# Last graph layer on column tiles of 32, with the mixing stage between the groups

## The chip, the cores and the metric

The kernel runs on one core of one Trainium2 chip. The metric is the device time of one execution in microseconds (us). Before the change the median of three runs is 4722.29 us (4718.48 to 4723.53). The engines are named as the profile does: PE is the matmul engine and PEld its weight loads, DVE is VectorE, ACT is ScalarE, POOL is GpSimd, SP issues DMAs. "PEclk" is the share of full speed that was granted to PE.

## The reference

A network of four layers over 3125 nodes with 256 features each. Every layer adds a graph part and a mixing part to x, and then an expert part. The change is in the last layer's graph part, which runs together with that layer's mixing part:

```python
def _L3_gnn_ref(x, edge_index, W, att_src, att_dst):      # 4 heads of 64 columns
    xp = (x @ W).reshape(n, 4, 64)
    a_src = jnp.einsum('nhc,hc->nh', xp, att_src)
    a_dst = jnp.einsum('nhc,hc->nh', xp, att_dst)
    e = leaky_relu(a_src[src] + a_dst[dst], 0.2)
    e_exp = jnp.exp(e - segment_max(e, dst)[dst])
    alpha = e_exp / segment_sum(e_exp, dst)[dst]
    return relu(segment_sum(alpha[:, :, None] * xp[src], dst).reshape(n, 256))

def _L3_mix_ref(x, Wq, Wk, Wv, Wm, W1, W2, g1, b1, g2, b2):
    Q, K = elu(q) + 1, elu(k) + 1                         # 8 heads of 32
    msg = layernorm(linear_attention(Q, K, v) @ Wm, g1, b1)
    h = relu(concat([x, msg]) @ W1) @ W2
    return x + layernorm(h, g2, b2)

xn = layernorm(x)
x = x + _L3_gnn_ref(xn, edge_index, ...) + _L3_mix_ref(xn[None], ...)[0]
x = x + _L3_ffn_ref(layernorm(x), ...)                    # one of 8 experts per node
```

## The kernel before

The nodes are 25 blocks of 125 (P), and also seven pieces (PIECES): six of 500 nodes (PW) and one of 125. `self.x`, `self.xn` and `self.xt` hold x, the normalised x, and the latter with features on partitions, for the whole network.

The graph part is done densely. Earlier, the kernel has written to HBM, for every piece of target nodes, a bf16 matrix of how often each source node points to each target (`ctt_d`). With exponentials taken apart into a factor of the source and one of the target, the weight of a source block for a stretch of targets is one ACT instruction and one DVE instruction: `t` = Relu(rows x scale + bias) on line 1951, and `z` = (t + us) x count on line 1954. `rows` holds, for each head, the targets' factor, the same on all partitions; `us` holds three factors of each source.

`l3_gnn_mix` (line 1834) sets this up. It makes the 64 columns of each head for each source block (`xr`, with a 65th column of ones, so that a product also gives the sum of the weights), the attention terms `al`, the bias, and `us`. It then runs two generators side by side in `together` (line 1892): `l3_dense`, the graph part, and `l3_mix_by_pieces`, the mixing part. At each turn the generator that is less far along goes on, so the program text of the two is interleaved in small steps. A scheduler then orders each engine's instructions by priority and readiness, mainly in that order[...].

`l3_dense` (line 1902) goes over four groups of pieces: three of two pieces (1000 targets) and the last piece alone. For each group

- it makes `rows`: for each head and piece two matmuls of a broadcast column of `wx` with `xt` (line 1930), and an Exp from PSUM into `xn`'s space (line 1932);
- for two heads at a time (for the last piece all four) it goes over the 25 source blocks. It loads the block's counts (`cs`, three buffers, two DMAs on SP, lines 155 and 156), makes `t` (two buffers) and `z` (three buffers) for each head, and issues one product per head and piece on line 1957: stationary `xr` (125 x 65), moving `z` (125 x 500), summed up in one PSUM bank per head and piece, four banks in all;
- it copies the four banks to SBUF, transposes them block by block (line 1972), and `finish` divides by the sum and adds the Relu to x with five DVE instructions per block and pair of heads (lines 1912 to 1919).

[...]

`l3_mix_by_pieces` (line 1990) first does keys and values of the 25 blocks (`keys_values`, lines 1270 to 1300), and then for each piece: queries, attention (line 1318), its normalising on DVE (lines 1322 to 1325), a transpose (line 1337), the product with Wm (line 254), a layer norm (`norm_piece`), a transpose (line 2021), W1 (line 2030), W2, a second layer norm, and the sum into x. Each piece needs several passes from PE to DVE or ACT and back.

When both parts of a piece are done, `arrive` starts its routing (`follow` in `l3_ffn`, line 2185): norm, transposes, gate products, softmax, slots, and a scattered write to HBM. The experts read this back after the last piece.

Of the kernel before, what the change touches and what calls it, by code (L numbers as in the profile page):

```python
# [12 lines left out]
F32 = mybir.dt.float32  # L13
# [4 lines left out]
AF = mybir.ActivationFunctionType  # L18
OP = mybir.AluOpType
# [4 lines left out]
N = 3125  # L24
D = 256
P = 125
NB = 25
HB = D // 128
# [9 lines left out]
PW = 500  # L38
# [67 lines left out]
PIECES = [(i, min(PW, N - i)) for i in range(0, N, PW)]  # L106


class Net:
# [1724 lines left out]
    def l3_gnn_mix(self, before, arrivals):  # L1834
# [5 lines left out]
        nc, a = self.nc, self.a  # L1840
        with ExitStack() as s:
            ms = s.enter_context(self.pool("m3_sb"))
            with self.pool("m3_w") as sb:
                w = self.load_w(sb, "L3_gnn_W")
                wx = self.attn_cols(sb, w, "wx", ["L3_gnn_att_src", "L3_gnn_att_dst"], ms)
            mix = self.l3_mix_by_pieces(ms, None)
# [4 lines left out]
            sb = s.enter_context(self.pool("g3_sb"))  # L1851
            wk = s.enter_context(self.pool("g3_wk", 2))
            pa = s.enter_context(self.pool("g3_ps", 1, space=PSUM))
            xr = sb.tile([P, NB, 4, 65], F32, name="xr")
            nc.gpsimd.memset(xr[:, :, :, 64:65], 1.0)
            al = sb.tile([P, NB, 8], F32, name="al")
            for b in range(NB):
                ps = self.bank()
                self.mm_tok(ps[:P, :264], self.xt, b, wx)
                nc.vector.tensor_copy(xr[:, b, :, :64], ps[:P, :D].rearrange("p (h d) -> p h d", h=4))  # L1860
                nc.scalar.copy(al[:, b, :], ps[:P, 256:264])
            m = sb.tile([P, 8], F32, name="m")
            nc.vector.tensor_reduce(m, al.rearrange("p b h -> p h b"), axis=AX.X, op=OP.max)
            ps = self.bank()
# [5 lines left out]
            ps = self.bank()  # L1870
# [4 lines left out]
            bias = sb.tile([P, 4], F32, name="bias3")  # L1875
# [5 lines left out]
            nc.vector.tensor_reduce(self.viol[:P, 6:7], over, axis=AX.X, op=OP.add)  # L1881
            nc.vector.tensor_tensor(bias, a8, bias, op=OP.min)

            us = sb.tile([P, 3, NB, 4], F32, name="us")
            nc.vector.tensor_sub(us[:, 2], al[:, :, :4], top[:, :, :4].to_broadcast([P, NB, 4]))
            nc.scalar.activation(us[:, 0], us[:, 2], AF.Exp)
            nc.scalar.activation(us[:, 1], us[:, 2], AF.Exp, scale=0.2)
            nc.vector.tensor_scalar(us[:, 2], us[:, 1], -1.0, None, op0=OP.mult)
            mix.send(mw)
            self.together([self.l3_dense(sb, wk, pa, wx, xr, us, bias), mix], (1.0, 1.15))  # L1890

    def together(self, parts, pace=(1.0, 1.0)):

# [5 lines left out]
            except StopIteration:  # L1899
                del at[p]  # L1900

    def l3_dense(self, sb, wk, pa, wx, xr, us, bias):

        nc = self.nc
        few = sb.tile([P, NB, 4], F32, name="few")
        free = self.xn.rearrange("p b d -> p (b d)")
        rows = free[:, :8 * PW].rearrange("p (h d) -> p h d", h=4)
        at = free[:65, 8 * PW:12 * PW].rearrange("p (h d) -> p h d", h=2)

        def finish(b, h0, nh, acc):  # L1910

            nc.vector.tensor_scalar(few[:, b, h0:h0 + nh], acc[:, :, 64], 1e-20, None, op0=OP.is_lt)
            rd = wk.tile([P, 4], F32, name="rd")
            nc.vector.tensor_scalar(rd[:, :nh], acc[:, :, 64], 1e-20, None, op0=OP.max)
            nc.vector.reciprocal(rd[:, :nh], rd[:, :nh])
            t = wk.tile([P, 4, 64], F32, name="tf")
            nc.vector.tensor_mul(t[:, :nh], acc[:, :, :64], rd[:, :nh, None].to_broadcast([P, nh, 64]))
            v = self.x[:, b, h0 * 64:(h0 + nh) * 64]
            nc.vector.scalar_tensor_tensor(v, t[:, :nh].rearrange("p h d -> p (h d)"), 0.0, v,
                                           op0=OP.max, op1=OP.add)  # L1920

        done, there = 0, []
        for p0 in range(0, len(PIECES), 2):
            pcs = PIECES[p0:p0 + 2]
            n = sum(w for _, w in pcs)
            for h in range(4):
                for k, (i, w) in enumerate(pcs):
                    ps = self.bank()
                    for c in range(HB):
                        nc.tensor.matmul(ps[:P, :w], wx[:, c, 260 + h:261 + h].to_broadcast([128, P]),  # L1930
                                         self.xt[:, c, i:i + w], start=(c == 0), stop=(c == HB - 1))
                    nc.scalar.activation(rows[:, h, k * PW:k * PW + w], ps[:P, :w], AF.Exp, bias=bias[:, h:h + 1],
                                         scale=0.8)
            hg = 4 if n < PW else 2
            for h0 in range(0, 4, hg):
                acc = {}
                for h in range(hg):
                    for k in range(len(pcs)):
                        acc[h, k] = pa.tile([65, 512], F32, name=f"acc{h * len(pcs) + k}")
                for b in range(NB):  # L1940
                    cs = wk.tile([P, 2, PW], BF, name="cs", bufs=3)
                    if len(pcs) == 2:
                        self.move(nc.sync, cs, self.ctt_d[p0:p0 + 2, :, b, :].rearrange("k p d -> p k d"))
                        c = cs.rearrange("p k d -> p (k d)")
                    else:
                        self.move(nc.sync, cs[:, 0, :n], self.ctt_d[p0, :, b, :n])
                        c = cs[:, 0, :n]
                    for h in range(hg):
                        k4 = h0 + h
                        t = wk.tile([P, 2 * PW], F32, name="t5")  # L1950
                        nc.scalar.activation(t[:, :n], rows[:, k4, :n], AF.Relu, bias=us[:, 2, b, k4:k4 + 1],  # L1951
                                             scale=us[:, 0, b, k4:k4 + 1])
                        z = wk.tile([P, 2 * PW], F32, name="z", bufs=3)
                        nc.vector.scalar_tensor_tensor(z[:, :n], t[:, :n], us[:, 1, b, k4:k4 + 1], c,  # L1954
                                                       op0=OP.add, op1=OP.mult)
                        for k, (i, w) in enumerate(pcs):
                            nc.tensor.matmul(acc[h, k][:, :w], xr[:, b, k4, :], z[:, k * PW:k * PW + w],  # L1957
                                             start=(b == 0), stop=(b == NB - 1))
                        done += n
# [5 lines left out]
                if hg == 2:  # L1965
                    for h in range(2):
                        for k, (i, w) in enumerate(pcs):
                            self.evac(at[:, h, k * PW:k * PW + w], acc[h, k][:, :w])
                    for j in range(n // P):
                        ps = self.bank()  # L1970
                        for h in range(2):
                            nc.tensor.transpose(ps[:P, h * 65:(h + 1) * 65], at[:, h, j * P:(j + 1) * P],
                                                self.ident[:65, :65])
                        finish(p0 * 4 + j, h0, 2, ps[:P, :130].rearrange("p (h c) -> p h c", h=2))
                        yield done / (NB * N * 4)
                else:
                    for h in range(4):
                        self.evac(at[:, h // 2, h % 2 * P:(h % 2 + 1) * P], acc[h, 0][:, :P])
                    ps = self.bank()
                    for h in range(4):  # L1980
                        nc.tensor.transpose(ps[:P, h * 65:(h + 1) * 65], at[:, h // 2, h % 2 * P:(h % 2 + 1) * P],
                                            self.ident[:65, :65])
                    finish(p0 * 4, 0, 4, ps[:P, :260].rearrange("p (h c) -> p h c", h=4))
# [426 lines left out]
```

## Time and profile before

| | |
|---|---|
| median of three runs | 4722.29 us |
| profiled execution | 4857.34 us, span 4855.5 us, mean PE clock 0.859 |
| PE busy in the span | 3791.1 us (78%) |
| DVE, ACT, POOL busy | 2518.8 (52%), 1321.2 (27%), 1016.0 us (21%) |
| product of the graph part, L1957 | first 3695.3, last 4586.5 us |
| t on ACT, L1951 | 400, median 1220 ns for 1000 columns |
| z on DVE, L1954 | 400, median 1258 ns for 1000 columns |
| cs loads | 150 of 218.8 KB and 150 of 25.4 KB for two pieces |

A time in a view is counted from the span's start. The page's groups give, for one line, engine and shape, the summed busy time, the mean duration of one, and the idle time before it with what ended it. Ends of matmuls are modelled and overlap the next one's start, so two neighbouring matmuls can have a mean duration that is longer than the distance between their starts. The stage of the change is the last fifth but one of the span; what follows it is the experts' stage.

### The profile page before, as it was taken

To read this page: it belongs to the slowest core of one execution; us is meant where nothing else is said; L and a number is where in the kernel's file an instruction comes from. 1 tells how busy PE (TensorE), PEld (TensorE's weight loads), DVE (VectorE), ACT (ScalarE), POOL (GpSimd) and SP (SyncE) were. 2 spreads that over 40 slices of the span, in tenths; PEclk is the share of its full clock that TensorE was granted. 3 is DMA by queue.
4 is the path that set the end of the run, shared out by engine and by line. 5 is a ranking of instruction groups with operands and counts; after the bars stand their busy time and mean duration, and the time that the engine had idled before them with its cause. 6 is when DMAs were issued, how large, how long until landed. Compare 5 with 4: busy or idle time off the path is not lost. (4 is left out here: it accounts for less than half of the span.)

```text
span 4855.5 us, 50596 instructions
## 1 busy us (share of the span) xinstructions
PE 3791.1 (78%) x16806; PEld 2521.4 (52%) x16806; DVE 2518.8 (52%) x8603; ACT 1321.2 (27%) x2364; POOL 1016.0 (21%) x1041
## 2 busy tenths in 40 slices
PE   1886895799657899997454556676599999999798
PEld 0675894566534565555343445455364444444465
DVE  5886335445576319954222222343355667667544
ACT  1466100111123232333000000000154655556511
POOL 1000002200243000002666666666000000000011
PEclk8786996799878799998676777787799999999799
DMA  6245511433230000002333333333301112111132
GB/s 181 59 119 145 137 33 40 127 119 118 82 80 19 24 14 7 14 7 65 90 94 92 93 92 92 86 93 92 111 7 31 51 44 59 42 49 52 50 128 68
DMA packets 253461, 352.56 MB, mean 73 GB/s; under 512 B 61645, under 2 KB 198276, under 8 KB 253191
## 3 DMA queue, kind: packets, MB, share of 16 engines
q1 hardware_dynamic: 133326, 169.77, 12.1%
q0 software_dynamic: 62832, 126.93, 9.9%
q10 hardware_dynamic: 57033, 52.54, 4.0%
q8 instruction: 137, 2.24, 0.2%
q14 instruction: 133, 1.09, 0.1%
HBM read 262.48 MB, written 94.92 MB: 74 GB/s over the span
## 5 line engine op out<-in xcount | busy, mean ns | idle before, releaser
L1598 POOL DMA_INDIRECT hg<-hx_d,idx x782 | 743.0, 950 | 418.8 <-issue 209.7
L1614 PE MATMUL acc<-hg,to 128*125 128x256 f32 x2042 | 590.7, 445 | 280.7 <-issue 157.7
L1614 PEld LDWEIGHTS acc<-hg,to 128*125 128x125 f32 x2042 | 439.3, 222 | 411.1 <-issue 192.7
L1957 PE MATMUL acc<-z,xr 125*65 125x500 f32 (+1 forms) x1400 | 573.7, 552 | 10.5 <-DVE z L1954 8.6
L1609 DVE TENSOR_SCALAR to<-iota_w,rel_b,kw 128x125 f32<-128x125 f32 (+1 forms) x782 | 252.7, 378 | 454.9 <-remote 263.6
L1954 DVE SCALAR_TENSOR_TENSOR z<-t,us,cs 125x1000 f32<-125x1000 f32 (+1 forms) x400 | 410.2, 1029 | 136.2 <-PE acc L1957 103.3
L1951 ACT ACTIVATE t<-xn,us 125x1000 f32<-125x1000 f32 (+1 forms) x400 | 409.4, 1037 | 236.9 <-DVE z L1954 231.3
L1957 PEld LDWEIGHTS acc<-z,xr 125*65 125x65 f32 x1400 | 187.8, 143 | 313.2 <-issue 271.3
L260 PE MATMUL ps<-xt,w 128*128 128x500 f32 (+1 forms) x672 | 268.8, 547 | 1.8 <-DMA w<-in_L_ffn_W_dram 1.8
L1533 DVE SCALAR_TENSOR_TENSOR junk<-iota_w,rel_b,lock 128x125 f32<-128x125 f32 (+1 forms) x782 | 248.0, 384 | 0.0
L796 ACT ACTIVATE k<-k 125x128 f32<-125x128 f32 x50 | 15.8, 317 | 775.1 <-DVE k L795 542.8
L2240 POOL DMA_INDIRECT bx_d<-row,slot x25 | 31.2, 1247 | 923.3 <-ACT t L1951 809.4
L588 PE MATMUL ps<-y,cb 125*125 125x256 bf16 x1875 | 215.2, 280 | 0.0
L588 PEld LDWEIGHTS <-cb 125*125 125x125 bf16 x1875 | 214.0, 141 | 0.1
L189 ACT ACTIVATE rstd_t<-rstd_t 125x4 f32<-125x4 f32 (+2 forms) x86 | 17.2, 203 | 678.6 <-DVE rstd_t L188 622.1
L254 PE MATMUL ps<-wo,h 128*125 128x256 f32 x800 | 187.7, 386 | 3.6 <-ACT h L1436 2.6
L1442 DVE SCALAR_TENSOR_TENSOR x<-ps,lg,x 125x256 f32<-125x256 f32 x200 | 92.7, 480 | 173.5 <-PE ps L254 173.5
L260 PEld LDWEIGHTS ps<-xt,w 128*128 128x128 f32 x672 | 122.7, 193 | 114.5 <-issue 102.2
L260 PE MATMUL ps<-h,w 128*128 128x500 f32 (+1 forms) x448 | 179.5, 541 | 2.3 <-ACT h L1431 1.6
L254 PEld LDWEIGHTS ps<-wo,h 128*125 128x125 f32 x800 | 142.7, 187 | 66.0 <-ACT h L1436 43.7
L260 PE MATMUL pl<-xbt,w 128*128 128x384 f32 x416 | 169.9, 557 | 8.2 <-DVE xbt L1152 5.8
L469 PE MATMUL t<-ky,lo 128*128 128x75 bf16 (+4 forms) x1251 | 138.5, 253 | 38.6 <-ACT ct L472 24.5
(566 smaller groups left out, 6225.3 us busy)
## 6 DMA issues: line engine op xcount, KB each, us to landing
cs<-ctt_d SPq DMA_DIRECT2D x150, 218.8 KB
w<-in_L_ffn_w_dram SPq DMA_DIRECT2D x52, 512.0 KB
cnt_d<-cd SPq DMA_DIRECT2D x25, 683.6 KB
cb<-cnt_d SPq DMA_DIRECT2D x25, 683.6 KB
ctt_d<-ct ACTq DMA_DIRECT2D x6, 2734.4 KB
hg<-hx_d,idx POOLq DMA_INDIRECT x782
b0x_d<-zero SPq DMA_DIRECT2D x1, 9984.0 KB
xb<-b0x_d SPq DMA_DIRECT2D x26, 384.0 KB
```

What stands on the lines that cost most here:

```text
L254: self.nc.tensor.matmul(ps, xt[:, h, b * P:(b + 1) * P], w[:, h, :], start=(h == 0), stop=(h == k - 1))
L260: self.nc.tensor.matmul(ps, w[:, h, :], xt[:, h, i:i + n], start=(h == 0), stop=(h == k - 1))
L469: nc.tensor.matmul(t[:, w * 25 * r:(w + 1) * 25 * r], lo[:, :, n % 4], ky[:, :25 * r, n % 4], start=(j == 0), stop=(j == ws[w0 + w][2] - 1))
L588: nc.tensor.matmul(ps[:P, :D], cf[k][:, h * P:(h + 1) * P], y3[:, b0 + k, j, :], start=(k == 0 and j == 0), stop=(k == m - 1 and j == 2))
L1442: nc.vector.scalar_tensor_tensor(self.x[:, b, :], ps[:P, :D], g[:, b, e:e + 1], self.x[:, b, :], op0=OP.mult, op1=OP.add)
L1533: nc.vector.scalar_tensor_tensor(junk[:, :m * P], self.iota_w[:, :m * P], rel[:, c:c + 1], lock[:, b:b + m].rearrange("p b n -> p (b n)"), ...
L1598: nc.gpsimd.indirect_dma_start(out=hg[:, j, :], out_offset=None, in_=hx, in_offset=bass.IndirectOffsetOnAxis(ap=idx[:, c0 + j:c0 + j + 1], ...
L1609: nc.vector.tensor_scalar(to, self.iota_w[:, :nb * P], rel[:, c:c + 1], kw[:, j:j + 1], op0=OP.is_equal, op1=OP.mult)
L1614: nc.tensor.matmul(acc[k], to[:, (k - b) * P:(k - b + 1) * P], hg[:, j, :D], start=(c == first[k]), stop=(c == last[k]))
L1951: nc.scalar.activation(t[:, :n], rows[:, k4, :n], AF.Relu, bias=us[:, 2, b, k4:k4 + 1], scale=us[:, 0, b, k4:k4 + 1])
L1954: nc.vector.scalar_tensor_tensor(z[:, :n], t[:, :n], us[:, 1, b, k4:k4 + 1], c, op0=OP.add, op1=OP.mult)
L1957: nc.tensor.matmul(acc[h, k][:, :w], xr[:, b, k4, :], z[:, k * PW:k * PW + w], start=(b == 0), stop=(b == NB - 1))
```

## The change

Seven things change, all in `l3_gnn_mix` and `l3_dense`.

1. `xr` has 64 columns; the column of ones goes. Each product is cut into tiles of 32 columns: for one source block, two heads and two pieces, eight products of 32 feature columns and four of 32 columns of ones (the sums). Each names its column tile with `tile_position=(0, q)`, q = 0, 32, 64, 96 in turn, and writes partitions q to q + 31 of a PSUM bank: one bank per piece (two heads of 64 columns), and one bank for the four sums.
2. These twelve products are chained with `add_manual_dep`, each after the one before it and the first after the block's `z`, and issued with `high_priority(5000)`. On PE the blocks of a group then follow one another; in the order of the changed kernel's instructions nearly all mixing and routing work stands between the groups.
3. A group takes three of four accumulator banks, turning on by three each time.
4. `rows` is no longer made on PE. Four Exp instructions on `al`, one transpose and one copy make the factors of all targets, which are written to HBM (`r_d`, 4 x 3125) and read back by broadcast, in `target_rows`: both head pairs ahead of the first group, and later each pair as soon as the group before has issued its last block.
5. `t` moves from its own two buffers to two stretches of `xn`'s space; `z` has four buffers in place of three; `at`, where results are copied, gets its own buffer.
6. The results are transposed as 128 x 125 tiles, four blocks to a bank, and `finish` works on four blocks at once.
7. The last piece, 125 targets wide, has all four heads in one group, also as twelve products of 32 columns per block.

```diff
-            xr = sb.tile([P, NB, 4, 65], F32, name="xr")
-            nc.gpsimd.memset(xr[:, :, :, 64:65], 1.0)
+            xr = sb.tile([P, NB, 4, 64], F32, name="xr")
...
+            r = sb.tile([P, 4, NB], F32, name="r3")
+            for h in range(4):
+                nc.scalar.activation(r[:, h], al[:, :, 4 + h], AF.Exp, bias=bias[:, h:h + 1], scale=0.8)
+            ps = self.bank()
+            nc.tensor.transpose(ps[:4 * NB, :P], r.rearrange("p h b -> p (h b)"), self.ident[:P, :P])
+            rt = sb.tile([4 * NB, P], F32, name="rt3")
+            nc.vector.tensor_copy(rt, ps[:4 * NB, :P])
+            r_d = self.dram.tile([4, N], F32, name="r3_d")
+            nc.sync.dma_start(r_d.rearrange("h (b p) -> (h b) p", p=P), rt)
...
+        spare = [free[:P, j * PW:(j + 2) * PW] for j in (8, 10)]
+        groups = [PIECES[p:p + 2] for p in range(0, len(PIECES), 2)]
+
+        def target_rows(g, h0):
+            if g < len(groups):
+                i, n = groups[g][0][0], sum(w for _, w in groups[g])
+                for h in (h0, h0 + 1):
+                    self.move(nc.sync, rows[:P, h, :n], r_d[h, i:i + n].partition_broadcast(P))
+
+        def finish(b, nb, h0, nh, acc):
+            w, nu = nb * P, len(acc) - 1
+            at = wk.tile([128, 3, PW], F32, name="at", bufs=1)
+            for k in range(nu + 1):
+                self.evac(at[:, k, :w], acc[k][:, :w])
...
+                for j in range(nb):
+                    nc.tensor.transpose(ps[:P, j * 128:(j + 1) * 128], at[:, k, j * P:(j + 1) * P], self.ident)
+                t = wk.tile([P, 4, 2, 64], F32, name="tf")
+                nc.vector.tensor_mul(t[:, :nb], ps[:P, :nb * 128].rearrange("p (j h d) -> p j h d", j=nb, d=64),
+                                     rd[:, :nb, 2 * k:2 * k + 2, None].to_broadcast([P, nb, 2, 64]))
...
-            for h in range(4):
-                for k, (i, w) in enumerate(pcs):
-                    ps = self.bank()
-                    for c in range(HB):
-                        nc.tensor.matmul(ps[:P, :w], wx[:, c, 260 + h:261 + h].to_broadcast([128, P]),
-                                         self.xt[:, c, i:i + w], start=(c == 0), stop=(c == HB - 1))
-                    nc.scalar.activation(rows[:, h, k * PW:k * PW + w], ps[:P, :w], AF.Exp, bias=bias[:, h:h + 1],
-                                         scale=0.8)
...
+            for hs in ((0, 2),) if len(pcs) == 1 else ((0,), (2,)):
+                units = [(h0, k, w) for h0 in hs for k, (_, w) in enumerate(pcs)]
+                acc = [pa.tile([128, 512], F32, name=f"acc{(turn + j) % 4}") for j in range(3)]
+                turn += 3
...
+                    zs, made = {}, made[-1:]
+                    for h in [h0 + j for h0 in hs for j in range(2)]:
+                        t = spare[h % 2]
+                        nc.scalar.activation(t[:, :n], rows[:P, h, :n], AF.Relu, bias=us[:, 2, b, h:h + 1],
+                                             scale=us[:, 0, b, h:h + 1])
+                        z = zs[h] = wk.tile([P, 2 * PW], F32, name="z", bufs=4)
+                        made.append(nc.vector.scalar_tensor_tensor(z[:, :n], t[:, :n], us[:, 1, b, h:h + 1], c,
+                                                                   op0=OP.add, op1=OP.mult))
-                        for k, (i, w) in enumerate(pcs):
-                            nc.tensor.matmul(acc[h, k][:, :w], xr[:, b, k4, :], z[:, k * PW:k * PW + w],
-                                             start=(b == 0), stop=(b == NB - 1))
+                    with self.tc.high_priority(5000):
+                        for out, left, h0, j, k, w, q in (
+                                [(acc[u], xr[:, b, h0 + j, f:f + 32], h0, j, k, w, 64 * j + f)
+                                 for u, (h0, k, w) in enumerate(units) for j in range(2) for f in (0, 32)]
+                                + [(acc[2], self.ones[:P, :32], h0, j, k, w, 64 * u + 32 * j)
+                                   for u, (h0, k, w) in enumerate(units) for j in range(2)]):
+                            mm = nc.tensor.matmul(out[q:q + 32, :w], left, zs[h0 + j][:, k * PW:k * PW + w],
+                                                  start=(b == 0), stop=(b == NB - 1), tile_position=(0, q))
+                            for i in made:
+                                self.tc.add_manual_dep(mm.ins, i.ins.name, row, reason="in one row")
+                            made = [mm]
...
+                for h0 in hs:
+                    target_rows(g + 1, h0)
+                finish(b0, pcs[0][1] // P, hs[0], 2 * len(hs), acc)
```

More of the change, by code (lines that the diff above doesn't have):

```diff
@@ L1859, in l3_gnn_mix @@
                 self.mm_tok(ps[:P, :264], self.xt, b, wx)
[L1860 removed]
+                nc.vector.tensor_copy(xr[:, b], ps[:P, :D].rearrange("p (h d) -> p h d", h=4))
                 nc.scalar.copy(al[:, b, :], ps[:P, 256:264])
@@ L1889, in l3_gnn_mix @@
             mix.send(mw)
-            self.together([self.l3_dense(sb, wk, pa, wx, xr, us, bias), mix], (1.0, 1.15))
+            self.together([self.l3_dense(sb, wk, pa, xr, us, r_d), mix], (1.0, 1.15))
     def together(self, parts, pace=(1.0, 1.0)):
@@ L1900, in together, with l3_dense @@
                 del at[p]
-    def l3_dense(self, sb, wk, pa, wx, xr, us, bias):
+    def l3_dense(self, sb, wk, pa, xr, us, r_d):
         nc = self.nc
@@ L1907, in l3_dense @@
         rows = free[:, :8 * PW].rearrange("p (h d) -> p h d", h=4)
[L1908 to L1920, printed above, removed]
@@ L1922, in l3_dense @@
-        done, there = 0, []
-        for p0 in range(0, len(PIECES), 2):
-            pcs = PIECES[p0:p0 + 2]
-            n = sum(w for _, w in pcs)
-            for h in range(4):
-                for k, (i, w) in enumerate(pcs):
-                    ps = self.bank()
-                    for c in range(HB):
-                        nc.tensor.matmul(ps[:P, :w], wx[:, c, 260 + h:261 + h].to_broadcast([128, P]),
-                                         self.xt[:, c, i:i + w], start=(c == 0), stop=(c == HB - 1))
-                    nc.scalar.activation(rows[:, h, k * PW:k * PW + w], ps[:P, :w], AF.Exp, bias=bias[:, h:h + 1],
-                                         scale=0.8)
[L1934 to L1939, printed above, removed]
+        spare = [free[:P, j * PW:(j + 2) * PW] for j in (8, 10)]
@@ new lines, in l3_dense @@
+        groups = [PIECES[p:p + 2] for p in range(0, len(PIECES), 2)]
[9 more added lines that the diff above has]
+                self.evac(at[:, k, :w], acc[k][:, :w])
+            ps = self.bank()
+            for j in range(nb):
+                nc.tensor.transpose(ps[:P, j * 128:(j + 1) * 128], at[:, nu, j * P:(j + 1) * P], self.ident)
+            sums = ps[:P, :nb * 128].rearrange("p (j q r) -> p j q r", j=nb, r=32)[:, :, :, 0]
+            rd = wk.tile([P, 4, 4], F32, name="rd")
+            f = wk.tile([P, 4, 4], F32, name="fw")
+            nc.vector.tensor_scalar(f[:, :nb], sums, 1e-20, None, op0=OP.is_lt)
+            nc.vector.tensor_scalar(rd[:, :nb], sums, 1e-20, None, op0=OP.max)
+            nc.vector.reciprocal(rd[:, :nb], rd[:, :nb])
+            for k in range(nu):
+                bk, hk = (b + 4 * k, h0) if nh == 2 else (b, 2 * k)
+                nc.vector.tensor_copy(few[:, bk:bk + nb, hk:hk + 2], f[:, :nb, 2 * k:2 * k + 2])
+                ps = self.bank()
+                for j in range(nb):
+                    nc.tensor.transpose(ps[:P, j * 128:(j + 1) * 128], at[:, k, j * P:(j + 1) * P], self.ident)
+                t = wk.tile([P, 4, 2, 64], F32, name="tf")
+                nc.vector.tensor_mul(t[:, :nb], ps[:P, :nb * 128].rearrange("p (j h d) -> p j h d", j=nb, d=64),
+                                     rd[:, :nb, 2 * k:2 * k + 2, None].to_broadcast([P, nb, 2, 64]))
+                v = self.x[:, bk:bk + nb, hk * 64:hk * 64 + 128]
+                nc.vector.scalar_tensor_tensor(v, t[:, :nb].rearrange("p j h d -> p j (h d)"), 0.0, v,
+                                               op0=OP.max, op1=OP.add)
@@ new lines, in l3_dense @@
+        done, there, turn, made = 0, [], 0, []
+        row = mybir.DependencyInfo(mybir.DependencyClass.NoSync, mybir.DependencyReason.DATA)
+        for h0 in (0, 2):
+            target_rows(0, h0)
+        for g, pcs in enumerate(groups):
+            b0 = pcs[0][0] // P
+            n = sum(w for _, w in pcs)
+            for hs in ((0, 2),) if len(pcs) == 1 else ((0,), (2,)):
+                units = [(h0, k, w) for h0 in hs for k, (_, w) in enumerate(pcs)]
+                acc = [pa.tile([128, 512], F32, name=f"acc{(turn + j) % 4}") for j in range(3)]
+                turn += 3
@@ L1942, in l3_dense @@
                     if len(pcs) == 2:
-                        self.move(nc.sync, cs, self.ctt_d[p0:p0 + 2, :, b, :].rearrange("k p d -> p k d"))
+                        self.move(nc.sync, cs, self.ctt_d[2 * g:2 * g + 2, :, b, :].rearrange("k p d -> p k d"))
                         c = cs.rearrange("p k d -> p (k d)")
                     else:
-                        self.move(nc.sync, cs[:, 0, :n], self.ctt_d[p0, :, b, :n])
+                        self.move(nc.sync, cs[:, 0, :n], self.ctt_d[2 * g, :, b, :n])
@@ L1947, in l3_dense @@
                         c = cs[:, 0, :n]
[L1948 to L1955, printed above, removed]
-                        for k, (i, w) in enumerate(pcs):
-                            nc.tensor.matmul(acc[h, k][:, :w], xr[:, b, k4, :], z[:, k * PW:k * PW + w],
-                                             start=(b == 0), stop=(b == NB - 1))
-                        done += n
+                    zs, made = {}, made[-1:]
@@ L1960, in l3_dense @@
+                    done += n * 2 * len(hs)
                     yield done / (NB * N * 4)
@@ L1964, in l3_dense @@
                         there = []
[L1965 to L1983, printed above, removed]
+                for h0 in hs:
+                    target_rows(g + 1, h0)
+                finish(b0, pcs[0][1] // P, hs[0], 2 * len(hs), acc)
+                yield done / (NB * N * 4)
             there = [i for i, w in pcs]
```

## The prediction

> **What bounds the kernel now.** The chain that ended last is no help here: it accounts for only some 7% of the span and breaks off inside the expert stage. So I read where TensorE (PE) is full (part 2 of the page), then the stage of the change by windows, then its groups with shapes kept apart, then single stretches of the timeline.
>
> ```profile
> PE   1886895799657899997454556676599999999798
> ...
> PEclk8786996799878799998676777787799999999799
> ```
>
> From slice 31 (3690 us) PE is full and its clock granted. The stage begins on PE at 3676.4, after L1871, and ends at 4610.2, at the first expert transpose. Columns below: stretch, its length, then busy us (instructions) of PE, PEld, DVE, ACT, POOL, PE clock, DMA share, GB/s.
>
> ```profile
> 3676.40:4610.20 933.80, 884.98 (x2771) 407.74 (x2771) 611.96 (x1335) 540.84 (x677) 31.18 (x25) 0.96 0.18 48
> 3690.00:4500.00 810.00, 796.71 (x2414) 353.41 (x2413) 543.29 (x1049) 471.94 (x536) 20.45 (x16) 1.00 0.19 50
> 4500.00:4610.20 110.20, 75.97 (x332) 48.93 (x331) 65.89 (x277) 63.21 (x131) 10.73 (x9) 0.70 0.16 42
> ```
>
> Up to 4500, PE idles 13 us in 810 at full clock, VectorE (DVE) is at 67%, ScalarE (ACT) at 58%: PE decides. After 4500 little dense work is left and 34 us are idle.
>
> ```profile
> L1957 PE MATMUL acc<-z,xr 125*65 125x500 f32 x1200 | 527.4, 583 | 2.8 <-DVE z L1954 2.8
> L1957 PE MATMUL acc<-z,xr 125*65 125x125 f32 x200 | 46.2, 367 | 7.7 <-DVE z L1954 5.8
> ...
> L1930 PE MATMUL ps<-xt,wx 128*125 128x500 f32 x78 | 36.3, 626 | 0.6 <-DVE rd L1914 0.6
> ...
> L1972 PE MATMUL ps<-ident,xn 65*125 65x65 f32 x96 | 15.1, 268 | 5.8 <-DVE few L1912 3.0 <-DVE rd L1914 1.3 <-DVE tf L1917 0.6
> ```
>
> The program has 700 products, the trace 1400 matmuls: each f32 product runs as two instructions, one behind the other. Their mean of 583 ns overlaps the next, so the price is the spacing:
>
> ```profile
> 4464.35 47.95 PE L1957 MATMUL acc<-z,xr 125*65 125x500 f32 x114
> ...
> 4470.77 2.64 DVE L1954 SCALAR_TENSOR_TENSOR z<-t,us,cs 125x1000 f32<-125x1000 f32 x2
> ```
>
> 47.95/114 = 0.42 us, so a product is 0.84 us and a block of two heads and two pieces (four products) 3.36 us. Where nothing holds DVE up, two z take 2.64 us: today they wait for PE.
>
> By spacing, the stage's 885 us of PE are: 150 full blocks x 3.36 = 504; 25 blocks of the last piece x 1.85 (46.2/25) = 46; rows of L1930, 96 x 0.42 + 16 x 0.21 = 44; 100 result transposes at 0.15 = 15; the remaining 276 are mixing and routing, which today fill gaps between dense products.
>
> **What the Trainium skill says.** "TensorE: Matmul & The Clock Gate", Part 3 (Measured speedup vs the span model): column tiles run side by side, three tiles with N=512 gave 2.38x, four row tiles 3.07x. The same part (What overlaps and what doesn't): matmuls start and end strictly in order. "TensorEngine Tiling (Array Packing)", Key Properties: a change of tiling mode drains TensorE. No run here shows tiles yet. The first page, HAM oscillation, lets PE's clock fall after pauses above about 3.4 us; the trace agrees: the first-layer mixing, which runs PE with pauses (14.27 us is the longest before L1337), had
>
> ```profile
> 1485.00:1540.00 55.00, 33.79 (x137) 22.42 (x137) 35.02 (x156) 15.93 (x28) 14.29 (x12) 0.84 0.08 17
> 1540.00:1600.00 60.00, 46.36 (x191) 33.25 (x190) 40.69 (x140) 15.46 (x27) 0.00 (x0) 0.72 0.00 1
> 1600.00:1670.00 70.00, 52.72 (x201) 37.25 (x200) 33.19 (x122) 18.58 (x33) 0.31 (x1) 0.67 0.14 42
> ```
>
> **The change part by part.**
>
> *Tiles.* A block becomes twelve products of 32 columns (eight of features, four of sums), issued to column tiles 0, 32, 64, 96 in turn: three rounds of four. If four run at once, a round costs one product: 3 x 0.84 = 2.51 us on PE. DVE then needs 2.64 for its two z, ACT 2 x 1.22 = 2.44, so DVE becomes the bound: 150 x 2.64 = 396, 108 less than 504. Bounds: 2.51 (PE alone) to 2.75 (t and z take turns on two buffers and their hand-over costs a little), that is -20 to +17 us. No row shows 24 weight loads of 32 columns in a block; the nearest spacing of load plus matmul is L469's 138.5 us/1251 = 0.11 us, so 24 x 0.11 = 2.66, no more than DVE. That tiles run at once is the assumption on which everything rests.
>
> *Last piece.* Its 25 blocks also become 24 short instructions: between 1.8 us (DVE's four z, 2 x 0.91 in the timeline near 4545) and 2.66. I take 2.3: 57 us against 46, +11.
>
> *Rows.* L1930's matmuls (44 us of PE), 28 Exp evictions and four table loads (5.1 us) on ACT go. In their place: four small Exp, one transpose, a copy, a 50 KB write and 16 broadcast reads (32 transfers, most rows 500 KB) through DRAM on SP's queue, read from r_d. At the 189 GB/s of 4600 to 4640 such a row takes 2.6 us. The first pair should be there at about 3690, while PE does six key-value blocks (2.25 us each, as in the first layer) that it had to do anyway: no loss. At later groups the reads wait for the last t of the group and stand ahead of the next cs loads on SP: 1.5 us of issue plus 1 MB, about 7 us, beside mixing work everywhere but between the first two groups. If mixing did not cover it: 5 x 7 = 35 us.
>
> *Results.* 100 transposes become 75 larger ones, 15 to 11 us; DVE's five small operations a block become few wide ones (some 20 us less, off the path). The fourth accumulator bank lets the next group start its first unit at once.
>
> *Order.* This is the cost. The instruction order of the changed kernel shows the 25 blocks of a group as one unbroken row on PE, and in the row DVE and ACT have almost only z and t. Mixing and routing stand between the groups: nothing after the first group but three key-value blocks, then thirteen, then whole pieces. There PE waits for each softmax, norm and copy, which before were hidden. What that costs is not in the trace; nearest is the first-layer mixing with routing, from 1506.0 to 1671.6: 166 us for work that at full-clock spacings (from the timeline, instructions x us) is about 97 (48 x 0.42 + 8 x 0.13, 100 x 0.222, 100 x 0.146, 100 x 0.13, 100 x 0.12, 25 x 0.15, 50 x 0.21), clock loss included: 11 us a piece of 500. The last layer's piece has two norms more. The first is on PE's path: statistics 0.6, two DVE steps, a table load 1.28, a root 0.2, four scalings of 0.54, about 4.6 us, and then a clock that may have fallen. I take 18 us a piece, 6.25 pieces: 113. Between 11 (70 us) and 25 (160 us). The start-up of t and z at six groups (6 x 2.5 us) about cancels with what still lies inside the rows of groups four, six and seven.
>
> *Sum.* PE 396 + 57 + 276 + 11 = 740; the 34 us of idle at the end stay; waits 113: 887 us against 934, -47 us. The profiled execution (4857.34 us: span 4855.5 and 1.84 around it) would become 4810. The median of the runs is 135 us lower; this stage was at full clock under the profiler, so I take the 47 off unscaled: **4675 us**. With its bounds (-43/+47 from the waits, -20/+17 from the block): 4615 to 4740.
>
> **The rivals.**
>
> *Pairs are not split (slower).* A product is two instructions on the same tile. If starts are strictly in order, the second waits for the first on its tile and holds back the next tile's; then only the tail of one product and the head of the next overlap, and each product costs 0.42. A block is 12 x 0.42 = 5.03 us: 150 x 2.39 = 358 more, 7 on the last piece: +318, 5040 us. For it: the fixed pairs in the trace and the skill's sentence on order. Against: the measured speedups are near the number of tiles. It decides from a block of 2.64 + 47/150 = 2.95 us on, that is, when fewer than 3.4 products run at once.
>
> *Tiles overlap partly.* At the skill's 3.07x a block is 12 x 0.84/3.07 = 3.28: +96, so 4770, slower too.
>
> *Mixing alone costs more.* At 30 us a piece (half clock after each pause) the waits are 190: 4752. It decides from 160 on.
>
> *The change doesn't do what it says:* excluded, the order shows the rows.
>
> **How the numbers follow.** Forecast 0.65, partial overlap 0.10, costlier mixing 0.09, pairs 0.16. The range 4620 to 4800 leaves out the pairs and a little below. The forecast's own range reaches past 4722, so of its 0.65 some 0.57 are faster by over 0.2% (9.4 us, about what a measurement of this kernel can tell), and edges of the next two add 0.03: faster 0.60, same 0.06, slower 0.34.
>
> **What would show it.** Tiles: matmuls of 32 columns that start within a few ns in fours, a group's row of 66 us (25 x 2.64), z waiting for t and no longer for PE. Pairs: a row of 126 us with DVE half idle. Rows: the first dense product near 3693. Order: PE idle and PEclk of 0.7 to 0.9 between the groups, about 18 us a piece. The forecast is wrong if a block takes over 2.95 us or the waits exceed 160 us.

## The result and the profile after

The changed kernel takes 4713.73 us (median of 20 runs, 4708.41 to 4719.77) against 4723.22 us (20 runs, 4713.42 to 4728.1) for the kernel before on the same chip: ratio 0.9983, 95% interval 0.9976 to 0.999. That is 9.5 us or 0.2% faster, where 47 us were forecast. A second comparison gave 0.9976 (0.9969 to 0.9982), 10.7 us. The profiled executions of the two kernels differ by 130 us already ahead of the stage of the change, in second-layer graph work that the diff doesn't touch, so their spans are not compared, only the stage itself.

First part 2 of the page after:

```profile
PE   1787796699928799999656566766799997997598
...
PEclk8786896699958789999877777887899998998699
```

The stage now begins at 3543.9 us (slice 31 of 40). Before, the slices of this stage were nearly all 9 in both rows until the end; now full slices alternate with slices of 7, 7 and 5 on PE and of 8, 8 and 6 on its clock.

The stage has the same two marks as before, the end of the matmul on `dg` and the first expert transpose. The windows view of the kernel after gives it twice, for L1991 alone (only PE and PEld have columns then) and for all instructions. Columns after the length: PE, PEld, DVE, ACT, POOL busy with counts, clock, DMA share, GB/s.

```profile
3543.90:4461.50 917.60, 437.19 (x4200) 143.25 (x4200) 0.89 0.21 56
...
3543.90:4461.50 917.60, 781.30 (x5436) 358.06 (x5437) 590.03 (x1151) 519.95 (x645) 29.98 (x25) 0.89 0.21 56
```

The same answer for the products of the kernel before, L1957 alone:

```profile
3676.40:4610.20 933.80, 573.66 (x1400) 187.81 (x1400) 0.96 0.18 48
```

The products fell from 574 to 437 us. Yet the stage fell only from 933.8 to 917.6, because PE's idle time rose from 49 to 136 us (length less PE busy) and the mean clock fell from 0.96 to 0.89. Of these 16 us the experts' stage behind gives 5 back (from 245.3 to 250.3 us, why was not followed up), which leaves 11, where the times give 9.5.

Where the time sits is seen in a walk through the stage of the kernel after, by windows: mixing, a row, mixing, mixing, a row, mixing, mixing, and the end.

```profile
3703.10:3734.30 31.20, 30.72 (x118) 16.22 (x118) 11.57 (x25) 14.96 (x43) 0.00 (x0) 1.00 0.09 22
3734.30:3800.40 66.10, 66.10 (x602) 21.70 (x601) 58.78 (x50) 57.38 (x49) 0.00 (x0) 1.00 0.38 101
3800.30:3852.90 52.60, 47.35 (x182) 27.75 (x182) 20.30 (x72) 16.83 (x35) 0.00 (x0) 1.00 0.06 14
3931.50:4025.40 93.90, 64.53 (x228) 41.13 (x230) 41.33 (x156) 21.09 (x35) 9.63 (x8) 0.76 0.09 24
4025.30:4091.40 66.10, 66.10 (x602) 21.70 (x601) 59.37 (x50) 57.82 (x49) 0.00 (x0) 1.00 0.35 90
4091.30:4174.90 83.60, 67.35 (x234) 41.05 (x235) 39.29 (x121) 21.97 (x35) 0.00 (x0) 0.88 0.06 19
4239.30:4334.90 95.60, 66.89 (x242) 42.29 (x243) 36.99 (x144) 20.22 (x34) 9.53 (x8) 0.77 0.02 2
4429.30:4461.50 32.20, 4.46 (x19) 3.68 (x18) 8.30 (x62) 3.65 (x6) 5.96 (x5) 0.50 0.24 78
```

An unbroken row of 25 blocks (below simply "a row"; the tensor of target factors is written `rows`) takes 66.1 us, 2.64 us a block, at full clock. The key-value blocks of the first stretch also keep PE full. But where whole pieces of mixing and routing stand alone, 94 us hold 64 us of PE work, and that work runs at a clock of 0.76. In this trace the granted clock has only two values, 1.0 and 0.5, so 0.76 is a mixture; two neighbouring windows inside this stretch show one each:

```profile
3949.90:3973.70 23.80, 19.22 (x61) 11.05 (x59) 4.32 (x14) 3.84 (x6) 3.46 (x3) 1.00 0.17 43
3973.80:3994.20 20.40, 9.51 (x32) 7.13 (x33) 12.60 (x51) 3.50 (x6) 0.15 (x1) 0.50 0.08 25
```

The groups of the kernel after, shapes kept apart, in the stage name the waits. The line below them is the first group again, in the stage of the kernel before, where one such matmul took 386 ns instead of 511:

```profile
L254 PE MATMUL ps<-L_mix_Wm,ot 128*125 128x256 f32 x100 | 35.4, 511 | 3.5 <-ACT ot L1338 3.0 <-DVE np_st L2075 0.3
...
L1337 PE MATMUL ps<-ident,o 125*128 125x125 f32 x50 | 14.0, 360 | 19.8 <-DVE o L1325 19.7
L2218 PE MATMUL ps<-ident,row 125*128 125x125 f32 x50 | 13.0, 376 | 42.0 <-DVE row L208 31.4 <-DVE row L2260 10.6
L2043 PE MATMUL ps<-ident,o 125*128 125x125 f32 x50 | 11.9, 389 | 13.1 <-DVE o L2080 13.1
...
L2239 PE MATMUL ps<-hot,before 125*125 125x32 f32 x12 | 3.6, 397 | 16.0 <-DVE hot L2235 16.0
```

```profile
L254 PE MATMUL ps<-L_mix_Wm,ot 128*125 128x256 f32 x100 | 24.1, 386 | 0.2
```

The normalising of the attention (L1325), the mixing norm (L2080), the routing norm (L208) and the routing compare (L2235) each hold PE up. The largest single wait between the groups, in the timeline of the kernel after (start, length, what, and in brackets the idle time before and what ended it):

```profile
3976.80 1.22 DVE L2060 TENSOR_TENSOR x<-x,o 125x1024 f32<-125x1024 f32 x1
...
3978.06 0.75 DVE L199 BATCH_NORM_STATS2 ln_st<-x 125x6 f32<-125x256 f32 x2
...
3980.50 1.38 DVE L208 TENSOR_SCALAR row<-x,ln_mv,ln_rs 125x256 f32<-125x256 f32 x4
3980.97 0.29 PEld L2218 LDWEIGHTS ps<-ident,row 125*128 125x128 f32 x2 [11.73 <-DVE row L208]
3980.97 0.68 PE L2218 MATMUL ps<-ident,row 125*128 125x125 f32 x2 [11.33 <-DVE row L208]
```

PE stands for 11.33 us behind one piece's last norm, its three wide DVE steps (L2060 is the last of them) and the routing's norm. The order of the kernel before laid dense products into such gaps.

The two waits next in size, 10.56 and 10.43 us, have another end. The second of them:

```profile
4261.74 1.38 DVE L208 TENSOR_SCALAR row<-x,ln_mv,ln_rs 125x256 f32<-125x256 f32 x4 [8.03 <-DMA bx_d<-row,slot]
...
4262.21 0.68 PE L2218 MATMUL ps<-ident,row 125*128 125x125 f32 x2 [10.43 <-DVE row L208]
```

Here the routing norm itself waits 8.03 us, until the scattered write of an earlier piece has landed and its buffer (`row`) is free; at the other one it is 7.00 us. So up to some 15 us of the 136 hang on a buffer of the routing. A kernel with more of these buffers was not run.

### The profile page after: what moved, and what is told of

It reads as the page before. It is cut to its first block, busy times and chain, and to the rows that moved or that the text cites. A ratio compares the mean times of both kernels' runs of the same rounds, so it can differ in the third digit from the quotient of the medians.

```text
span 4711.8 us, 55745 instructions
## 1 busy us (share of the span) xinstructions
PE 3676.7 (78%) x19470; PEld 2480.6 (53%) x19470; DVE 2486.9 (53%) x8419; ACT 1300.2 (28%) x2332; POOL 1014.6 (22%) x1040
## 5 line engine op out<-in xcount | busy, mean ns | idle before, releaser
L1614 PE MATMUL acc<-hg,to 128*125 128x256 f32 x2042 | 577.8, 445 | 200.9 <-DVE to L1609 192.6
L1614 PEld LDWEIGHTS acc<-hg,to 128*125 128x125 f32 x2042 | 450.7, 225 | 310.5 <-DVE to L1609 216.0
L1982 DVE SCALAR_TENSOR_TENSOR z<-xn,us,cs 125x1000 f32<-125x1000 f32 (+1 forms) x400 | 398.1, 1028 | 68.1 <-PE acc L1991 39.7
L1979 ACT ACTIVATE xn<-xn,us 125x1000 f32<-125x1000 f32 (+1 forms) x400 | 403.9, 1038 | 87.8 <-DVE z L1982 86.2
L1991 PE MATMUL acc<-z,xr 125*32 125x500 f32 (+1 forms) x2800 | 416.7, 551 | 3.8 <-DVE z L1982 2.4
L1602 DVE TENSOR_TENSOR kw<-hg,awt 128x8 f32<-128x8 f32 x98 | 16.4, 167 | 583.9 <-DMA hg<-hx_d,idx 522.5
L1991 PE MATMUL acc<-z,ones 125*32 125x500 f32 (+1 forms) x1400 | 276.9, 546 | 0.0
L1991 PEld LDWEIGHTS acc<-z,xr 125*32 125x32 f32 x2800 | 107.6, 111 | 228.2 <-DVE z L1982 126.0
L242 PE MATMUL ps<-ident,xn 125*128 125x125 f32 x300 | 57.9, 343 | 159.1 <-DVE xn L208 159.0
```

The costliest lines, as they stand in the source:

```text
L242: self.nc.tensor.transpose(ps[:, j * P:(j + 1) * P], src[:, i // P + j, h * 128:(h + 1) * 128], self.ident[:P, :P])
L1614: nc.tensor.matmul(acc[k], to[:, (k - b) * P:(k - b + 1) * P], hg[:, j, :D], start=(c == first[k]), stop=(c == last[k]))
L1979: nc.scalar.activation(t[:, :n], rows[:P, h, :n], AF.Relu, bias=us[:, 2, b, h:h + 1], scale=us[:, 0, b, h:h + 1])
L1982: made.append(nc.vector.scalar_tensor_tensor(z[:, :n], t[:, :n], us[:, 1, b, h:h + 1], c, op0=OP.add, op1=OP.mult))
L1991: mm = nc.tensor.matmul(out[q:q + 32, :w], left, zs[h0 + j][:, k * PW:k * PW + w], start=(b == 0), stop=(b == NB - 1), tile_position=(0, q))
```

## The experiments

Each kernel is compared with the kernel before that was measured beside it: 4855.03 us (4848.54 to 4860.41) for the first four, 4721.94 us for whole rounds, whole blocks and the kernel with few sums, 4724.72 us for the other three. In the expectations "G" is the theory that the order between the groups gives back what the tiles gain; "M", where it stands, is its rival.

**Rows through DRAM alone.** The kernel before, with `r3_d` and the broadcast reads in place of L1930 and its Exp:

```
-                        nc.tensor.matmul(ps[:P, :w], wx[:, c, 260 + h:261 + h].to_broadcast([128, P]),
-                                         self.xt[:, c, i:i + w], start=(c == 0), stop=(c == HB - 1))
-                    nc.scalar.activation(rows[:, h, k * PW:k * PW + w], ps[:P, :w], AF.Exp, bias=bias[:, h:h + 1],
-                                         scale=0.8)
...
+                    self.move(nc.sync, rows[:P, h, :m], r_d[h, i:i + m].partition_broadcast(P))
```

> The kernel before, with the rows made once, written to HBM and read back by broadcast, as the change does; no tiles, old order. Theory G: PE loses 44 us of matmuls that nothing hid: about 4682 us, less a few us where a group waits for its rows. If the reads hold up the groups: 4710 us or more, with z waiting for a DMA or t for the rows at six group starts.

Measured: 4815.49 us, ratio 0.9928 (0.9905 to 0.9951), 40 us faster, with 24 to 46 us in the interval; by the two marks the stage is some 33 us shorter (901.2 for 933.8). The removed matmuls were 44 us of PE. No wait of ScalarE for the reads of `r_d` shows in this trace, and 0.7 us of it in the kernel after.

**The order alone.** The kernel before, its products of 65 columns put ahead of everything on PE:

```
-                        for k, (i, w) in enumerate(pcs):
+                        with self.tc.high_priority(5000):
+                            for k, (i, w) in enumerate(pcs):
```

> The kernel before, with its products of 65 columns issued with high_priority(5000): its order becomes that of the changed kernel, with mixing between the groups, but no tiles. Theory G: the order alone costs what the changed kernel pays, 100 to 130 us: about 4840 us, with PE idle and its clock at about 0.76 between the groups. If the order is free and something else takes the gain: within 15 us of 4723.

Measured: 5002.14 us, ratio 1.0301 (1.0284 to 1.0318), 147 us slower, more than expected. The windows of this kernel: its stage, and two stretches of it.

```profile
3679.40:4755.70 1076.30, 938.01 (x2773) 431.43 (x2773) 626.17 (x1335) 552.78 (x679) 29.97 (x25) 0.91 0.15 42
...
3770.00:3860.00 90.00, 90.00 (x216) 30.20 (x215) 63.96 (x53) 63.81 (x59) 0.00 (x0) 1.00 0.25 69
...
4180.00:4280.00 100.00, 73.21 (x247) 46.21 (x248) 39.97 (x179) 18.90 (x32) 9.66 (x8) 0.81 0.06 16
```

The same picture without any tile: rows at full clock, mixing with gaps at 0.81. Idle time is 138 us and the clock 0.91, as in the changed kernel. So it is the order that costs, with or without tiles.

**The changed kernel without its priority.** Once with the order inside a block kept, once without:

```
-                    with self.tc.high_priority(5000):
+                    with ExitStack():
```

and in the second also

```
-                            for i in made:
-                                self.tc.add_manual_dep(mm.ins, i.ins.name, row, reason="in one row")
-                            made = [mm]
```

> The changed kernel without high_priority(5000): the twelve products of a block keep their chain, but mixing and routing may stand between and inside the blocks again. Theory G (given back): the tiles' gain is real and the order between the groups gives it back as waits and as a lower clock. Then PE has 403 + 33 us of tiles and 287 of the rest at full clock, plus 264 changes of tiling mode at about 0.09 us, and idles about 40 to 60 us: a stage of 790 to 810 us against 917, so about 4595 us. Theory M (mode changes): mixing between the groups was the cheaper way, because a change of tiling mode among mixed work costs far more than 0.09 us; at 0.5 us each the 264 changes take 130 us, and the time is 4700 us or more.

> The changed kernel without the priority and without the chain of manual dependencies (282 changes of mode in place of 264, products of different blocks may mix). Theory G: within 15 us of the kernel with the chain alone, about 4600 us. Theory M: slower than that kernel, 4710 us or more.

Measured: 4804.0 us, ratio 0.9895 (0.9878 to 0.9911), 51 us faster than before; and 4798.38 us, 0.9895 (0.9876 to 0.9913). The order inside a block makes no difference to the time that these runs show; giving up the unbroken rows gains some 40 us on the changed kernel. But far less came than expected. The stage of the first, products alone and all:

```profile
3677.90:4556.30 878.40, 499.80 (x4200) 144.41 (x4200) 0.95 0.22 59
...
3677.90:4556.30 878.40, 804.32 (x5437) 336.61 (x5437) 579.59 (x1151) 513.77 (x643) 31.96 (x25) 0.95 0.22 59
```

Idle is down to 74 us and the clock up to 0.95, as the theory has it, but the products went from 437 to 500 us. The timeline of PE in this kernel suggests a reason:

```profile
3918.09 5.45 PE L254 MATMUL ps<-L_mix_W,hid 128*125 128x256 f32 x24
3923.47 1.02 PE L1991 MATMUL acc<-z,xr 125*32 125x500 f32 x2
3924.42 1.99 PE L254 MATMUL ps<-L_mix_W,hid 128*125 128x256 f32 x8
```

One product (two matmuls) stands alone between two mixing products: it takes 0.95 us from its start to the next one's, where a round of four in a row takes 0.84. A round that is broken up loses its neighbours.

**Whole rounds, whole blocks.** The priority is taken from the first product of each round (in the second kernel: of each block), so that mixing can come in ahead of it and hardly anywhere else:

```
-                    with self.tc.high_priority(5000):
...
+                        with self.tc.high_priority(5000) if q else ExitStack():
```

and for whole blocks

```
+                        with self.tc.high_priority(5000) if q or out is not acc[0] else ExitStack():
```

> Only the first product of each round of four has no priority, so mixing can come between rounds but not inside one: 7 rounds are broken in PE's order instead of 78 in the version without priority. Theory 'the order gives the tiles' gain back, and in the version without priority broken rounds did the rest': 71 fewer lone products at 0.84 us are 60 us less than that version: stage 815 to 825 us, 105 to 115 us under the kernel before (ratio 0.977). Rival 'each change between tiles and the whole array costs, wherever it stands': the number of changes is the same (135 stretches against 133), so the time is that of the version without priority, 50 us under before (0.9895).

> As the version with whole rounds, but mixing can come in only between blocks of twelve products (109 stretches instead of 135). Theory 'broken rounds': no rounds to gain, 26 fewer changes at 2 x 0.09 us are 5 us, against PE's waits for z inside a block that nothing can fill any more: within 10 us of the version with whole rounds. Rival 'each change costs': better than that by a fifth of the whole loss, 15 us or more.

Measured: 4652.26 us, ratio 0.9858 (0.9843 to 0.9873), 70 us faster than before; and 4636.54 us, 0.982 (0.9807 to 0.9833), 85 us. The stages, whole rounds first:

```profile
3539.20:4396.70 857.50, 483.41 (x4200) 138.76 (x4200) 0.94 0.22 60
...
3539.20:4396.70 857.50, 787.78 (x5436) 331.93 (x5436) 579.56 (x1151) 512.03 (x643) 33.07 (x25) 0.94 0.22 60
```

```profile
3544.00:4382.50 838.50, 474.21 (x4200) 139.65 (x4200) 0.95 0.23 61
...
3544.00:4382.50 838.50, 770.52 (x5436) 329.13 (x5436) 576.09 (x1151) 511.79 (x643) 32.40 (x25) 0.95 0.23 61
```

Broken rounds fell from 78 to 7 (so the instruction order has it), and the stage by 21 us (19 by the times), not by the 60 expected: they were a part of the loss. The rival, a price for each change between tiles and whole array, had expected no gain in this step, and 15 us or more in the next, which brought 16 by the times and 19 by the stages. Both hold in part, and the sizes of neither were right. Whole blocks is the mirror of the changed kernel: the same products and the same mixing, with idle time of 68 us for 136 and the rest of PE's work at 296 us for 344, against 37 us more in the products. The net is 79 us by the stages and 75 by the times, and that is what the unbroken rows cost.

**t and z earlier, mixing earlier.** On top of whole blocks: t and z ahead of mixing on ACT and DVE; then instead the pace of the two parts changed:

```
-                        nc.scalar.activation(t[:, :n], rows[:P, h, :n], AF.Relu, bias=us[:, 2, b, h:h + 1],
-                                             scale=us[:, 0, b, h:h + 1])
+                        with self.tc.high_priority(400):
+                            nc.scalar.activation(t[:, :n], rows[:P, h, :n], AF.Relu, bias=us[:, 2, b, h:h + 1],
+                                                 scale=us[:, 0, b, h:h + 1])
...
+                        with self.tc.high_priority(400):
+                            made.append(nc.vector.scalar_tensor_tensor(z[:, :n], t[:, :n], us[:, 1, b, h:h + 1], c,
+                                                                       op0=OP.add, op1=OP.mult))
```

```
-            self.together([self.l3_dense(sb, wk, pa, xr, us, r_d), mix], (1.0, 1.15))
+            self.together([self.l3_dense(sb, wk, pa, xr, us, r_d), mix], (1.0, 1.5))
```

> Whole blocks, and t and z moved ahead of mixing's steps on ScalarE and VectorE. If PE's waits for z inside the blocks are what keeps that version's products at 467 us where whole rounds need 410 (150 x 2.51 + 33): up to 50 us faster than it. If mixing's steps are then late for PE instead (an engine's time is only moved): the same within 10 us, or slower.

> Whole blocks, and mixing's steps stand earlier in program order beside the dense blocks (pace 1.5 for 1.15). If the stage's end, with PE at half use and a clock of 0.7 to 0.8 for its last 140 us, is mixing left over after the dense work: 10 to 30 us faster than whole blocks. If it is the routing and the small products of the last piece, which wait for the dense results anyway: the same within 10 us.

Measured: 4638.79 us, ratio 0.9821 (0.9808 to 0.9834), the same as whole blocks; and 4626.66 us, 0.9795 (0.9782 to 0.9808), 98 us faster than before and the best of all. In the first the products fell from 474 to 461 us and idle rose from 68 to 73, mixing's part of PE from 296 to 309: the time moved to another engine's steps, as its rival said. The second took about 10 us off whole blocks, the low end of what its theory gave and at the edge of what the two intervals can tell apart; 6 us of it are in the stage (838.5 to 832.6). So most of the tail is probably not left-over mixing.

**Is a row bound by z or by TensorE?** The changed kernel with the four products on ones only in blocks 0 and 24, so that it leaves out most of the sums (the thresholds of the sums, also changed, are not shown):

```
-                                   for u, (h0, k, w) in enumerate(units) for j in range(2)]):
+                                   for u, (h0, k, w) in enumerate(units) for j in range(2) if b in (0, NB - 1)]):
```

> Leaves out most of the sums: the four products with ones only in blocks 0 and 24, so that the results are not normalised (thresholds of the sums set so that nothing divides by zero). If VectorE's z sets the pace of a row (forecast): PE has two rounds a block instead of three (1.68 us instead of 2.51), but the row of 25 blocks stays at 64 to 66 us and the kernel within 10 us of the changed one. If PE's rounds set it (four tiles not quite side by side): the row falls by 23 x 0.8 = 18 us to about 48 us, and the kernel by 100 us.

Measured: 4656.11 us, ratio to before 0.9867 (0.9852 to 0.9882), 55 us under the changed kernel, between the two expectations. The time can't answer, because with fewer products mixing came to stand inside the rows (186 stretches of products on PE, 36 in the changed kernel), so two things changed. A stretch of unbroken blocks in it still can (windows, then groups of the same stretch):

```profile
4174.30:4191.80 17.50, 16.05 (x109) 3.61 (x108) 16.69 (x23) 15.65 (x13) 5.17 (x4) 1.00 0.39 101
```

```profile
L1982 DVE SCALAR_TENSOR_TENSOR z<-xn,us,cs 125x1000 f32<-125x1000 f32 x13 | 16.4, 1263 | 0.1
L1991 PE MATMUL acc<-z,xr 125*32 125x500 f32 x108 | 16.1, 591 | 1.4 <-DVE z L1982 1.4
```

108 matmuls, 16 to a block, are 6.75 blocks in 17.5 us: 2.59 us a block with two rounds instead of three, z without a gap on DVE and PE waiting for it. With three rounds a block takes 2.64 us, so the sums are all but hidden beside z. But z alone is not the bound of the changed kernel's row. In the row from 4025.3 to 4091.4 it waits too, and mostly for products that hold its buffers:

```profile
L1982 DVE SCALAR_TENSOR_TENSOR z<-xn,us,cs 125x1000 f32<-125x1000 f32 x49 | 59.6, 1257 | 6.7 <-PE acc L1991 4.9 <-ACT xn L1979 0.9
```

Two z are 2.51 us, three rounds are 2.51 us, and a block takes a little more than either.

**The order of the tiles.** The changed kernel with a block's twelve products sorted by tile:

```
-                                [(acc[u], xr[:, b, h0 + j, f:f + 32], h0, j, k, w, 64 * j + f)
+                                sorted([(acc[u], xr[:, b, h0 + j, f:f + 32], h0, j, k, w, 64 * j + f)
...
+                                   for u, (h0, k, w) in enumerate(units) for j in range(2)], key=lambda p: p[6])):
```

> The changed kernel with the twelve products of a block sorted by tile (three on tile 0, then three on 32, 64, 96) instead of going round. If what runs side by side is only what stands side by side in the order: the next tile's first product starts with the last of the tile before, a block takes 4 x 2 x 0.84 = 6.7 us, a row of 25 some 168 us, and the kernel is 610 us slower than the changed one. If TensorE takes products of other tiles past a waiting one: rows of 66 us as before.

Measured, one run: 4851.05 us, 126 us above the kernel before, so about 137 above the changed kernel, which lies 10.7 under it. One of its rows, by windows:

```profile
3772.80:3860.60 87.80, 87.80 (x602) 31.04 (x601) 58.84 (x50) 57.58 (x49) 0.00 (x0) 1.00 0.30 79
```

That is 3.51 us a block, (3.51 - 2.64) x 150 = 131 of the 137 us. Neither expectation came true: in the trace three matmuls start together every 0.43 us, always one with ones and two with `xr`. The trace does not name the tiles, but ones is the third product of its tile and the two others are earlier ones, so three neighbouring tiles, one product apart, would give this picture. Read so, TensorE does go past a product whose tile is taken, but only so far.

## Why the prediction was wrong

The direction was right and the size was not: 9.5 us for 47. The step that failed is the one the prediction called the cost, "Order", and in its sum the term of the waits: 18 us a piece, 113 us. It was to hold the lower clock as well, and left almost no room for it: waits and clock together came to 159 us. Set against the sum of the stage, from the windows above:

| term | forecast | measured |
|---|---|---|
| six groups of 25 blocks | 396 | 402 (437.2 - 35.3) |
| last piece's 25 blocks | 57 | 35.3 |
| mixing, routing and results on PE | 287 | 344 (781.3 - 437.2) |
| PE idle: the end 34, waits 113 | 147 | 136 |
| stage | 887 | 917.6 |

*Tiles: right.* Four products do run side by side. The trace of the kernel after, starts of successive matmuls of the first block of a row:

```
4025.283 4025.290 4025.298 4025.303   4025.728 4025.734 4025.741 4025.748   4026.147 ...
```

Four start within 20 ns and the next four 0.42 to 0.45 us later; a block is 2.64 us, the value taken. Its reason was half right: one of the signs named was z "waiting for t and no longer for PE", and in the row z waits 4.9 us for PE and 0.9 for t. That PE's 2.51 us and z's 2.51 lie so close made the value come out all the same. The rivals of split pairs (5.03) and partial overlap (3.28) are refuted. The Trainium skill's 2.38x for three column tiles ("TensorE: Matmul & The Clock Gate", Part 3) is 0.79 of the number of tiles; here 12 products of 0.84 us in 2.64 us are 3.8 at once, 0.95 of four. The sentence on strict order that the prediction quotes does not hold between tiles here: the second half of the first product starts 0.43 us after the first halves of the three products behind it.

*Last piece: over-priced by 22 us.* PE was busy 35.3 us on its products, in a stretch of 94 us that mixing shares. The upper bound had priced 24 weight loads one behind the other; 35.3/25 = 1.4 us a block shows that they overlap, at 24 x 0.11 us alone they would be 2.6.

*`rows` through DRAM: right.* 40 us alone by the times, 33 by the stage, against 44 us of PE; the first product starts 19 us into the stage, as forecast (17).

*Order: the mechanism right, the size not.* The idle time came out as summed: less the 34 us that the end was to have it is 102 us, 16 us a piece. The missing part is the clock. The waits were to include the clock's loss, and mixing's work was put into the sum at full clock, 287 us; it took 344. At the full-clock spacing of each shape its 1236 matmuls are about 288 us of work, as summed; those that started while the clock stood at 0.5 are about 57 us of it, and they took up to twice as long (0.84 us for 0.42 from one matmul of 500 columns to the next). So waits and clock are 102 + 57 = 159 us, 25.5 a piece: the upper end of the prediction's own bounds and all but the point from which it said the third rival decides (160). That rival named the form of it, half clock after a pause, though its 30 us a piece are too many. That most of the 57 us are the order's doing is shown by whole blocks, where the same work is 296 us at a clock of 0.95, 48 us less. Of the 18 us a piece that were taken, the idle time alone used 16, which left 2 for the clock where 9 were needed (57/6.25); the first layer's windows ahead of the forecast, with 0.84, 0.72 and 0.67, had already shown such clocks.

*The sum of parts.* `rows` alone gave 40 us, the order alone cost 147, the whole gave 9.5; if these add up, the tiles brought about 117 in this order, 108 in the forecast. No run has the tiles alone, and what they bring depends on the order: taking off the same 40 us for `rows`, about 11 us remain where mixing may come in anywhere (51) and about 45 in whole blocks (85). A saving on PE and a loss of cover were each larger than the result. The error of 46 us in one term, less the 22 us that the last piece gave back by luck, and with 6 us more for the blocks, made the stage 31 us longer than forecast; with the 5 us of the experts' stage that is most of the missing 37.5.

## What to carry to other kernels

A product that fills the engine is also the cover for everything that waits; when it is made faster or moved into one row, price the work that loses its cover at the clock and the waits that it shows alone, not at the clock it has while covered. Tiles that run side by side must be kept together in order, but no further than needed: keeping each block whole and letting other work in between the blocks gave 85 us where one row of 25 blocks gave 10. Test such a change in parts, since its effects here were +147, -40 and, by difference, about -117 us.

## What was not expected of the hardware

- Four fp32 products on four column tiles keep each tile's own pace: starts 7 ns apart, each tile's next 0.42 us later.
- With products sorted by tile three products still run at once (3.51 us a block, three starts every 0.43 us).
- One product of 32 columns between whole-array products costs 0.95 us, no less than a whole round of four (0.84 us in a row).
- The granted clock stood at 1.0 or at 0.5 and nothing between: 0.76 in a stretch of mixing is a mixture, in which neighbouring matmuls of 500 columns start either 0.42 or 0.84 us apart.
- The change from whole-array products to tiles is small in itself: from the last mixing matmul of a stretch to the first tile product were 0.51 us (4024.77 to 4025.28) where the spacing without a change is 0.42.
